# Fewer, differently shaped side transfers in the recurrent layer of a four-layer graph network

## The chip, the cores and the metric

The kernel runs on one core of a Trainium2 chip. The metric is device time in microseconds (us) of one execution. Before the change it is 3273.84 us, the median of three runs (3273.52 to 3274.08).

## The reference, cut to what matters

The network takes x (64 graphs, 256 nodes, 256 features) and adj (64 x 256 x 256), in float32, and applies four layers, each of the form x = layernorm(x + layer(x)). Only layer 0 is touched by the change. It is a recurrence over the 256 nodes: the state of a node is computed from the states that are there, and replaces its row before the next node is computed.

```python
d = jnp.sum(adj, axis=-1)
dinv = jnp.where(d != 0, 1.0 / jnp.where(d != 0, d, 1.0), 0.0)
norm_adjT = jnp.swapaxes(adj, 1, 2) * dinv[:, :, None]
def step(h, i):
    x = jnp.take(h_e, i, axis=1)
    row = jnp.take(norm_adjT, i, axis=1)
    x_par = jnp.einsum('bj,bjd->bd', row, h)
    iou = x @ W_ioux.T + b_ioux + x_par @ W_iouh.T + b_iouh
    r, z = jnp.split(iou, 2, axis=1)
    r, z = (jax.nn.sigmoid(r), jax.nn.sigmoid(z))
    hc = jnp.tanh(x @ W_coux.T + b_coux + x_par * r @ W_couh.T + b_couh)
    h_new = z * x_par + (1.0 - z) * hc
    h = jax.lax.dynamic_update_slice(h, h_new[:, None, :], (0, i, 0))
    return (h, None)
```

So each step needs, for each of the 64 graphs, a weighted sum x_par over all nodes: original features for nodes from here on, new states for nodes already done. Layers 1 to 3 (a graph convolution and two attention layers) follow.

## The kernel before, in words

`_recurrence` is layer 0, and `_layers` runs the other three. The 256 steps are one Python loop, `for now in range(N)`, unrolled into an instruction list whose order is written out by hand: every engine, and the queue of SyncE (SP), executes its instructions in exactly the order of the program. n is the step, p = n % 8 its place in a group of eight (U = 8), k and i = divmod(n, 32) its block of 32 (T = 32) and the place in it. State tiles hold two halves of the features (256 = 2 x 128) over 64 graphs, so 128 partitions.

**The chain of a step.** The weighted sum xp is transposed (`flip`, L627 on TensorE, L629 on ScalarE), multiplied with the weights (`h_part`, L620), goes through the sigmoid (L861, used here as the mark at which a step begins), a transpose and a product (L863, L865), a second product, tanh (L898), zcc (L900), and ends in the next xp (L903). Everything else is fitted beside this chain.

**The weighted sum** of a step is assembled in a tile ACC of its group from five sources:
- the original features: products of x_side, written to HBM (Us) and loaded by `sums_in` (L316, at p = 1);
- the recent states: VectorE adds them one by one (`push`, L645) or ScalarE and GpSimd in groups (`scale_far`, L687 to L696);
- the window of states before that: `late`. States are kept in a ring Hw (128 partitions, one for each of 64 recent nodes and half of the graphs), written by `into_ring` (L672 to L676), two transfers a state. At p = 0 to 3 of a group, TensorE multiplies Hw with a table An (L531), ScalarE copies the products into lb (L256), and lb goes to HBM and back into another partition order: `send` (L511, two transfers Lb<-lb) and `receive` (L517, late_sb<-Lb). GpSimd adds late_sb to the ACC of the next group at p = 6 and 7 (L909);
- older states: `early`. Blocks of states are flushed to HBM (`flush`, L655, Hd<-Hw, at i = 8 and 16), loaded again together with adj, multiplied at p = 4 to 7 (L424), copied into a tile eu, and stored: `store` (L436, two transfers Es<-eu), called by `at_step` one step after the last copy. `early_in_part` (L453) loads them at p = 0 for the group after the next, as one transfer of 128 partitions x 8 x 128, and GpSimd adds them at p = 3 and 4 (L855);
- the node's own value, with a table Sd.

**Tables.** While block k runs, the tables of k + 1 are prepared: `degrees` loads rows of adj (L301, two transfers of 256 KB each time) and sums them on VectorE (L304, two reductions for each load), called as a generator at the values of i in a tuple; `late_load` loads a raw table from adj (at most four transfers for a block) and GpSimd cuts An out of it at n + 15 to 23; `load_S` loads S.

**The queue.** All transfers of the loop go through SP's one in-order queue, at the end of each step: first those filed under this step by `at_step` (`transfers`), then `early_in_part`, `sums_in`, the next x (xq), flush, degrees, raw and S, and, at p < 4, up to two loads from the list `loads` (`load_later`, `next_load`, L269), sorted by a rank. The ring inserts are issued in the middle of a step, at p = 4 to 7: at most two states a step, that is, four transfers:

```python
if p > 3 or n >= N - U:
    for _ in range(min(2, len(ring_in))):
        into_ring()
```

The `late` products of a group at p = 0 read the ring with the states of the group before it, up to the one that is finished at the start of p = 7; that one is in the last two transfers of p = 7.

Of the kernel before, what the change touches and what calls it, by code (L numbers as in the profile page):

```python
# [9 lines left out]
F32 = mybir.dt.float32  # L10
# [9 lines left out]
P = 128  # L20
# [50 lines left out]
def _recurrence(tc, ident, Hd, x, adj, W_ioux, b_ioux, W_iouh, b_iouh, W_coux, b_coux, W_couh, b_couh, wide, then):  # L71
# [19 lines left out]
    nc = tc.nc  # L91
    B, N, D = x.shape
    T = 32
# [10 lines left out]
    with ExitStack() as ctx:  # L104
# [149 lines left out]
        def copy_later(out, in_, then=None):  # L254
            def f(n):
                nc.scalar.copy(out, in_)  # L256
                held.pop(0)
                if then:
                    then(n)

            copies.append(f)
# [118 lines left out]
        def early_load(n, k, lo, hi, t):  # L380

            rows = hi - lo
            if (k, lo) not in Es:
                Es[k, lo] = dram.tile([2, NG, 4, T, P], F32, name=f"Es_{k}_{lo}", bufs=1)
            if not any(e[0] == (hi, t) for e in states_in):
                Hs = wide.tile([P, GB, D], F32, tag="wide", name=f"Hs_{hi}_{t}")
                states_in.append(((hi, t), Hs, load_later(
                    Hs[0:rows], Hd[lo:hi, t * GB:(t + 1) * GB, :], 1
                )))
            _, Hs, begun = next(e for e in states_in if e[0] == (hi, t))  # L390
            if t % 2 == 0:
                A = stream.tile([P, 2 * GB, T], F32, tag="A", name=f"A_{k}_{lo}_{t}")
                early_A[:] = A, load_later(
                    A[0:rows],
                    adj[t * GB:(t + 2) * GB, lo:hi, k * T:(k + 1) * T].rearrange("b j i -> j b i"), 1
                )
            early_in.append(((begun, early_A[1]), k, lo, hi, t, Hs, early_A[0]))
# [14 lines left out]
        def early_fill(n):  # L412

            if early_pb:
                pb, e = early_pb.pop(), 1
            else:
                if not early_in or not landed(early_in[0][0], n):
                    return False
                _, k, lo, _, t = early_in[0][0:5]
                pb, e = base_bank([P, 2, D], f"early_{k}_{lo}_{t}"), 0  # L420
                early_pb.append(pb)
            _, k, lo, hi, t, Hs, A = early_in[0]
            for q in range(4):
                nc.tensor.matmul(  # L424
                    pb[q * T:(q + 1) * T, e, :], A[0:hi - lo, t % 2 * GB + e * 4 + q, :],
                    Hs[0:hi - lo, e * 4 + q, :], start=True, stop=True,
                )
            if e:
                early_in.pop(0)
                if t % 2 == 0:  # L430
                    early_ub[:] = [stream.tile([P, 4, D], F32, tag="ub", name=f"eu_{k}_{lo}_{t}")]
                ub = early_ub[0]

                def store():
                    for c in range(2):
                        nc.sync.dma_start(  # L436
                            Es[k, lo][c, 2 * t - 2:2 * t + 2].rearrange("n q i f -> (q i) n f"),
                            ub[:, :, c * P:(c + 1) * P],
                        )

                copy_later(
                    ub[:, t % 2 * 2:t % 2 * 2 + 2, :], pb,
                    (lambda n: at_step(n + 1, store)) if t % 2 else None,
                )
            return True

        def early_in_part(first):

            k, i = divmod(first, T)
            for (kk, lo), E in Es.items():  # L450
                if kk == k:
                    part = blk.tile([P, U, P], F32, tag="early", name=f"early_sb_{first}_{lo}")
                    nc.sync.dma_start(  # L453
                        part, E[:, :, :, i:i + U, :].rearrange("c n q i f -> (c n q) i f")
                    )
                    early_parts.append((first, part))

        early_parts = []

        def late_load(k, n=None):  # L460


            An = blk.tile([P, HB, U, T // U], F32, tag="An", name=f"An_{k}")
            raw = stream.tile([P, HB, T], F32, tag="raw", name=f"raw_{k}", bufs=1)
            first, last = k * T - W + T // 2, k * T + T // 2
            if first < 0:
                nc.gpsimd.memset(raw, 0.0)
            begun = []
            for lo, hi, at in ring(max(first, 0), last):
                for g in range(2):  # L470
                    to = raw[g * W + at:g * W + at + hi - lo]
                    of = adj[g * HB:(g + 1) * HB, lo:hi, k * T:(k + 1) * T].rearrange(
                        "b j i -> j b i"
                    )
                    if n is None:
                        nc.scalar.dma_start(to, of)
                    else:
                        begun.append(load_later(to, of, 1.5))

            def begin():  # L480
                while not all(begun):
                    next_load(now)

            def cut(lo):
                part = raw[:, lo:lo + HB // 4].rearrange("p b (s u) -> p b s u", u=U)
                take = window[k % 2].rearrange("p (s u) -> p s u", u=U).unsqueeze(1)
                nc.gpsimd.tensor_mul(
                    An[:, lo:lo + HB // 4].rearrange("p b u s -> p b s u"), part,
                    take.to_broadcast(list(part.shape)),
                )  # L490

            if n is not None:
                at_step(n + 12, begin)
            for e in range(4):
                if n is None:
                    cut(e * HB // 4)
                else:
                    at_step(n + (15, 18, 21, 23)[e], lambda e=e: cut(e * HB // 4))
            return An

        def late(first):

            k, i = divmod(first, T)
            An = tables[k]["An"]
            lb = stream.tile([P, NG, D], F32, tag="lb", name=f"lb_{first}", bufs=1)
            Lb = dram.tile([2, NG, 4, U, P], F32, tag="Lb", name=f"Lb_{first}")
            sides[first] = blk.tile([P, U, P], F32, tag="late", name=f"late_sb_{first}", bufs=1)

            def send():
                for c in range(2):  # L510
                    nc.sync.dma_start(  # L511
                        Lb[c].rearrange("n q u f -> (q u) n f"),
                        lb[i // U::T // U, :, c * P:(c + 1) * P],
                    )

            def receive():
                nc.sync.dma_start(sides[first], Lb.rearrange("c n q u f -> (c n q) u f"))  # L517
# [6 lines left out]
            for u in range(0, NG // 2, 2):  # L524
                pb = [base_bank([P, 2, D], f"late_{first}_{u}_{g}") for g in range(2)]
                for e in range(2):
                    for q in range(4):
                        for g in range(2):
                            rows = slice(g * W, (g + 1) * W)
                            b = (u + e) * 4 + q  # L530
                            nc.tensor.matmul(  # L531
                                pb[g][q * T:(q + 1) * T, e, :],
                                An[rows, b].rearrange("p u s -> p (u s)"),
                                Hw[rows, b, :], start=True, stop=True,
                            )
                    if e:
                        for g in range(2):
                            at = g * NG // 2 + u
                            copy_later(
                                lb[:, at:at + 2, :], pb[g],  # L540
                                then if g and u + 2 == NG // 2 else None,
                            )
                    n = yield
# [157 lines left out]
        sums = {}  # L701
        sides = {}
        xqT = {}
        pushes = []
        ring_in = []

# [42 lines left out]
        warm = work.tile([P, P], F32, tag="ready", name="warm", bufs=1)[:, 0:1]  # L749
        nc.vector.memset(warm, 0.0)  # L750
        nc.scalar.activation(warm, warm, AF.Sigmoid)
        tables[0]["An"] = late_load(0)
        tables[0]["Sd"] = chain_S(0)
        for a in range(1, 3):
# [38 lines left out]
        for now in range(N):  # L793
# [10 lines left out]
            if n:  # L804
# [11 lines left out]
                    behind = [(n - 1, hs, m, 4) for m in range(end, min(end + U, N), 4)]  # L816

                if p > 3 or n >= N - U:
                    for _ in range(min(2, len(ring_in))):
                        into_ring()  # L820
            if p == 0 and U < n + U < N:
                late_side = late(n + U)
# [109 lines left out]
            if k + 1 < NB:  # L932
                if i == 0:
                    background = degrees(k + 1)
                for _ in range((0, 2, 3, 3, 8, 10, 11, 15, 16, 17, 20, 21, 23, 24).count(i)):
                    next(background, None)
                if i == 0:
                    tables[k + 1]["S"], double = load_S(k + 1, n)
                    at_step(n + 19, double)
                    tables[k + 1]["An"] = late_load(k + 1, n)  # L940
                if i == 28:
                    tables[k + 1]["Sd"] = chain_S(k + 1)
            if p < 4:
# [623 lines left out]
```

## Time and profile before

| what | us |
|---|---|
| time, median of three runs | 3273.84 |
| the profiled execution | 3276.55 |
| its span in the profile | 3274.8 |
| steps of the recurrence, first to last sigmoid (L861) | 137.1 to 1432.9 |
| TensorE busy in the span | 3071.4 |
| VectorE, ScalarE, GpSimd busy in the span | 2587.5, 1990.7, 1881.9 |

The profile is of one execution. A line of a view names an engine, a line of the kernel and the tile written and read, for instance "late<-Hw,An". SPq is the queue of SP; its lines are issues of transfers, whose data land later. In a timeline the columns are start, duration, engine, line, operation and tiles, a count, and in brackets how long the engine stood idle before and what ended it. In a table of windows each row is a stretch of time: its length, the busy time of TensorE, of its weight loads, of VectorE, ScalarE and GpSimd, with counts of instructions, then TensorE's clock, the mean busy share of the 16 DMA engines, and GB/s.

A step takes about 5.6 us at p = 0, 5.2 at p = 4 and 4.4 to 4.7 elsewhere; 38.8 us for an undisturbed group of eight.

### The profile page before, as it was taken

The numbers are of one execution on the slowest core, as the hardware profiler recorded it, in microseconds if no ns is written. First come the engines' busy times: TensorE is split into PE (matmuls) and PEld (weight loads), VectorE is DVE, ScalarE is ACT, GpSimd is POOL, SyncE is SP. The second block draws the span as 40 slices with busy tenths as digits, with TensorE's granted clock in tenths as the row PEclk, the third lists the DMA queues.
The fourth block names the chain that finished last, engine by engine and source line by source line (L and its number), as shares of the span: only waits on it lengthen the run. The fifth ranks groups of instructions, "written<-read, shape, count | busy, mean of one in ns | idle before, by whom it ended". The sixth has DMA issues, their size and how long they took to land.

```text
span 3274.8 us, 80656 instructions
## 1 busy us (share of the span) xinstructions
PE 3071.4 (94%) x28332; PEld 2275.9 (69%) x28332; DVE 2587.5 (79%) x7361; ACT 1990.7 (61%) x5224; POOL 1881.9 (57%) x2226
## 2 busy tenths in 40 slices
PE   4799999999899989959999999999999999999997
PEld 3566666555565555647888888888888888888885
DVE  2477777777678778756888988888888888888885
ACT  0266666666566656635666666666666666666664
POOL 2366767766677778733555555555555555555543
PEclk8899999999999999978999999999999999999999
DMA  9866777687776764433333333333333333333310
GB/s 297 258 163 148 188 176 185 166 180 183 175 184 148 181 152 139 100 72 70 78 78 78 78 78 78 78 78 78 78 78 78 78 79 77 79 77 78 78 43 21
DMA packets 806736, 385.77 MB, mean 118 GB/s; under 512 B 525260, under 2 KB 774232, under 8 KB 802648
## 3 DMA queue, kind: packets, MB, share of 16 engines
q1 hardware_dynamic: 788312, 362.61, 46.4%
q10 hardware_dynamic: 18016, 17.96, 1.7%
q8 instruction: 227, 3.72, 0.5%
q14 instruction: 181, 1.48, 0.2%
HBM read 261.75 MB, written 99.61 MB: 110 GB/s over the span
## 4 chain that ended last, share of the span: by engine, by line
PE 82%; DMA 7%; DVE 6%; issue 2%; SPq 2%; POOL 1%; ACT 1%; ACTq 0%; DVEq 0%; POOLq 0%
PE mm L1044 14%; PE rc L620 7%; PE rc L612 5%; PE s L1270 4%; PE late L531 4%; PE mm_3v L1044 4%; PE mm_2f L1044 4%; PE mm_2v L1044 3%; PE mm_3f L1044 3%; PE mm_t L1044 3%; PE mm_g L1044 3%; PE mm_2s L1044 3%; PE mm_2w L1044 3%; PE o L1305 3%; PE z_ps L620 2%; PE z_ps L612 2%
## 5 line engine op out<-in xcount | busy, mean ns | idle before, releaser
L1282 POOL TENSOR_TENSOR p3s<-p 128x256 f32<-128x256 f32 x512 | 358.4, 732 | 269.5 <-ACT p L1280 269.3
L1044 PE MATMUL mm<-xT,weights 128*128 128x256 f32 x2048 | 485.4, 385 | 2.7 <-ACT xT L1160 2.7
L696 POOL TENSOR_TENSOR ACC<-ACC,far 128x640 f32<-128x640 f32 (+2 forms) x312 | 412.8, 1323 | 69.8 <-ACT far L687 26.1
L645 DVE SCALAR_TENSOR_TENSOR ACC<-keep,S,ACC 128x128 f32<-128x128 f32 x1561 | 436.8, 343 | 13.0 <-POOL ACC L909 8.2
L1044 PEld LDWEIGHTS mm<-xT,weights 128*128 128x128 f32 x2048 | 387.1, 192 | 80.4 <-ACT xT L1160 29.3
L1279 DVE TENSOR_TENSOR p<-s,neg 128x512 f32<-128x512 f32 x512 | 317.7, 683 | 84.8 <-PE s L1270 84.8
L1000 ACT ACTIVATE y<-y,shift,rstd 128x256 f32<-128x256 f32 x512 | 279.6, 596 | 158.2 <-DVE shift L998 158.1
L1280 ACT ACTIVATE p<-p 128x512 f32<-128x512 f32 x512 | 307.0, 629 | 3.1 <-DVE p L1279 3.0
L612 PE MATMUL rc<-WxT,xqT 128*64 128x256 f32 x2048 | 271.8, 387 | 2.2 <-ACT xqT L256 2.2
L842 POOL TENSOR_TENSOR ready<-ACC,dinv 128x128 f32<-128x128 f32 x255 | 101.8, 399 | 279.6 <-DVE ACC L645 275.1
L992 POOL TENSOR_TENSOR rstd<-rstd,mhalf 128x2 f32<-128x2 f32 x256 | 173.5, 695 | 134.2 <-DVE rstd L991 132.4
L692 POOL TENSOR_TENSOR far<-hs,S 128x384 f32<-128x384 f32 (+1 forms) x310 | 222.0, 716 | 4.7
L1319 DVE RECIPROCAL rT<-o 128x256 f32<-128x256 f32 x128 | 223.7, 1748 | 0.0
L988 DVE BATCH_NORM_STATS2 st<-y 128x6 f32<-128x256 f32 x512 | 209.6, 409 | 12.7 <-POOL y L1181 9.9
L1192 ACT ACTIVATE qk<-mm,weights 128x256 f32<-128x256 f32 x256 | 107.5, 471 | 164.1 <-PE mm L1044 162.2
L1181 POOL TENSOR_TENSOR y<-y,g 128x512 f32<-128x512 f32 x64 | 81.1, 1267 | 216.7 <-ACT g L1178 190.2
L531 PE MATMUL late<-Hw,An 64*32 64x256 f32 x3840 | 166.3, 402 | 35.7 <-DMA Hw<-hs 21.5
L620 PE MATMUL rc<-WhT,rT 128*64 128x128 f32 x2048 | 172.3, 290 | 26.2 <-DVE rT L865 24.5
L620 PE MATMUL rc<-WhT,xpT 128*64 128x128 f32 x2048 | 170.9, 288 | 25.7 <-ACT xpT L629 24.5
L620 PEld LDWEIGHTS rc<-WhT,rT 128*64 128x64 f32 x2048 | 109.0, 138 | 123.7 <-DVE rT L865 102.5
L687 ACT ACTIVATE far<-hs,S 128x128 f32<-128x128 f32 x534 | 183.7, 397 | 3.1 <-POOL ACC L696 0.8
L620 PEld LDWEIGHTS rc<-WhT,xpT 128*64 128x64 f32 x2048 | 107.8, 137 | 106.1 <-ACT xpT L629 95.7
(170 smaller groups left out, 7307.8 us busy)
## 6 DMA issues: line engine op xcount, KB each, us to landing
xX<-in_x_dram ACTq DMA_DIRECT2D x16, 1024.0 KB
Us<-xu SPq DMA_DIRECT2D x64, 256.0 KB
ACC<-Us SPq DMA_DIRECT2D x32, 512.0 KB
Es<-eu SPq DMA_DIRECT2D x64, 256.0 KB
early_sb<-Es SPq DMA_DIRECT2D x32, 512.0 KB
xin<-in_x_dram SPq DMA_DIRECT2D x64, 256.0 KB
ad<-in_adj_dram SPq DMA_DIRECT2D x64, 256.0 KB
y<-Hd SPq DMA_DIRECT2D x64, 256.0 KB
```

Of the source, the lines that this page charges most:

```text
L531: nc.tensor.matmul(pb[g][q * T:(q + 1) * T, e, :], An[rows, b].rearrange("p u s -> p (u s)"), Hw[rows, b, :], start=True, stop=True,)
L612: nc.tensor.matmul(G[o * B:(o + 1) * B], xqT[a, i // 2][:, i % 2, kc, h * B:(h + 1) * B], WxT[:, kc, o, gates], start=False, stop=False, s ...
L620: nc.tensor.matmul(G[o * B:(o + 1) * B], hT[:, kc * B:(kc + 1) * B], WhT[:, kc, o, g], start=False, stop=(kc == 1), skip_group_check=True,)
L645: nc.vector.scalar_tensor_tensor(acc[:, 0, :], keep[:, j % 2, :], s, acc[:, 0, :], ALU.mult, ALU.add)
L692: nc.gpsimd.tensor_mul(tmp[:, begun:count, :], hs.unsqueeze(1).to_broadcast(shape), s[:, begun:count].unsqueeze(2).to_broadcast(shape),)
L696: nc.gpsimd.tensor_add(acc, acc, tmp[:, 0:count, :])
L1000: nc.scalar.activation(y[:, c, :], y[:, c, :], AF.Identity, bias=shift[:, c:c + 1], scale=rstd[:, c:c + 1],)
L1044: nc.tensor.matmul(pm[:, c, :], lhsT[:, k, c * P:(c + 1) * P], rhs[:, k, :], start=(k == 0), stop=(k == 1),)
L1279: nc.vector.tensor_add(p, s_ps[i], self.neg3)
L1280: nc.scalar.activation(p, p, AF.Exp, scale=ISQ)
L1282: nc.gpsimd.tensor_add(both, p[:, 0, :], p[:, 1, :])
L1319: nc.vector.reciprocal(rT, o_ps[:, 1, :])
```

## The change

Five edits, all in layer 0's side work:
1. lb and eu are laid out as [2 halves][units][128] rather than [units][256], so that the two transfers of `send` and of `store` become one each, with the same bytes. The copies on ScalarE write into the new layout.
2. Es in HBM is laid out in the order [pair of units][half][4][4][32][128]. `early_in_part` becomes two transfers of 64 partitions each, one for each half. The outermost dimension of each source is the 4 of the pairs.
3. `store` is filed one step later when its last copy falls in a step with p = 5 (p = 7 rather than 6).
4. The raw table is loaded by a function of its own, `raw_load`, called at i = 24 of the block before (n = 0 for the second block), rather than at i = 0; of the four loads of degree rows in a block, the second moves from i = 3 to i = 8, and its two reductions from i = 8 and 10 to i = 10 and 11; the third load stays at i = 11.
5. Ring inserts take up to 3, 3, 1 and 1 states at p = 4, 5, 6 and 7, rather than two each time.

```diff
-                Es[k, lo] = dram.tile([2, NG, 4, T, P], F32, name=f"Es_{k}_{lo}", bufs=1)
+                Es[k, lo] = dram.tile([NG // 4, 2, 4, 4, T, P], F32, name=f"Es_{k}_{lo}", bufs=1)
...
-                    early_ub[:] = [stream.tile([P, 4, D], F32, tag="ub", name=f"eu_{k}_{lo}_{t}")]
+                    early_ub[:] = [stream.tile([P, 2, 4, P], F32, tag="ub", name=f"eu_{k}_{lo}_{t}")]
...
                 def store():
-                    for c in range(2):
-                        nc.sync.dma_start(
-                            Es[k, lo][c, 2 * t - 2:2 * t + 2].rearrange("n q i f -> (q i) n f"),
-                            ub[:, :, c * P:(c + 1) * P],
-                        )
-
+                    nc.sync.dma_start(
+                        Es[k, lo][t // 2].rearrange("c n q i f -> (q i) (c n) f"),
+                        ub.rearrange("p c n f -> p (c n) f"),
+                    )
+
+                at = t % 2 * 2
                 copy_later(
-                    ub[:, t % 2 * 2:t % 2 * 2 + 2, :], pb,
-                    (lambda n: at_step(n + 1, store)) if t % 2 else None,
+                    ub[:, :, at:at + 2, :].rearrange("p c n f -> p n c f"),
+                    pb.rearrange("p n (c f) -> p n c f", c=2),
+                    (lambda n: at_step(n + (2 if n % U == 5 else 1), store)) if t % 2 else None,
                 )
...
                     part = blk.tile([P, U, P], F32, tag="early", name=f"early_sb_{first}_{lo}")
-                    nc.sync.dma_start(
-                        part, E[:, :, :, i:i + U, :].rearrange("c n q i f -> (c n q) i f")
-                    )
+                    for c in range(2):
+                        nc.sync.dma_start(
+                            part[c * B:(c + 1) * B],
+                            E[:, c, :, :, i:i + U, :].rearrange("e n q i f -> e (n q) i f"),
+                        )
...
-            lb = stream.tile([P, NG, D], F32, tag="lb", name=f"lb_{first}", bufs=1)
+            lb = stream.tile([P, 2, NG, P], F32, tag="lb", name=f"lb_{first}", bufs=1)
...
             def send():
-                for c in range(2):
-                    nc.sync.dma_start(
-                        Lb[c].rearrange("n q u f -> (q u) n f"),
-                        lb[i // U::T // U, :, c * P:(c + 1) * P],
-                    )
+                nc.sync.dma_start(
+                    Lb.rearrange("c n q u f -> (q u) (c n) f"),
+                    lb[i // U::T // U].rearrange("p c n f -> p (c n) f"),
+                )
...
-                    for _ in range(min(2, len(ring_in))):
+                    for _ in range(min((3, 3, 1, 1)[p - 4] if n < N - U else 2, len(ring_in))):
                         into_ring()
...
-                for _ in range((0, 2, 3, 3, 8, 10, 11, 15, 16, 17, 20, 21, 23, 24).count(i)):
+                for _ in range((0, 2, 3, 8, 10, 11, 11, 15, 16, 17, 20, 21, 23, 24).count(i)):
                     next(background, None)
                 if i == 0:
+                    if not k:
+                        raw_load(1, n)
                     tables[k + 1]["S"], double = load_S(k + 1, n)
                     at_step(n + 19, double)
                     tables[k + 1]["An"] = late_load(k + 1, n)
+                if i == 24 and k + 2 < NB:
+                    raw_load(k + 2, n)
```

More of the change, by code (lines that the diff above doesn't have):

```diff
@@ L452, in early_in_part, with raw_load @@
                     part = blk.tile([P, U, P], F32, tag="early", name=f"early_sb_{first}_{lo}")
-                    nc.sync.dma_start(
-                        part, E[:, :, :, i:i + U, :].rearrange("c n q i f -> (c n q) i f")
-                    )
+                    for c in range(2):
[3 more added lines that the diff above has]
+                        )
                     early_parts.append((first, part))
         early_parts = []
-        def late_load(k, n=None):
-            An = blk.tile([P, HB, U, T // U], F32, tag="An", name=f"An_{k}")
+        def raw_load(k, n=None):
             raw = stream.tile([P, HB, T], F32, tag="raw", name=f"raw_{k}", bufs=1)
@@ L478, in late_load @@
                         begun.append(load_later(to, of, 1.5))
+            raws[k] = raw, begun
+        def late_load(k, n=None):
+            An = blk.tile([P, HB, U, T // U], F32, tag="An", name=f"An_{k}")
+            raw, begun = raws.pop(k)
             def begin():
@@ L539, in late @@
                             copy_later(
-                                lb[:, at:at + 2, :], pb[g],
+                                lb[:, :, at:at + 2, :].rearrange("p c n f -> p n c f"),
+                                pb[g].rearrange("p n (c f) -> p n c f", c=2),
                                 then if g and u + 2 == NG // 2 else None,
@@ L703, in _recurrence @@
         xqT = {}
+        raws = {}
         pushes = []
@@ L751, in _recurrence @@
         nc.scalar.activation(warm, warm, AF.Sigmoid)
+        raw_load(0)
         tables[0]["An"] = late_load(0)
```

## The prediction

> **What bounds the kernel now.** I read the page first, then the waits, then one stalled group in the timelines of TensorE and SP, then the DMA share by step.
>
> Only layer 0 changes, 1296 us from its first to its last sigmoid. TensorE is nearly always busy there, but each step is a chain through TensorE, ScalarE and VectorE, so what counts is how far a step is over its normal length. I took the time between sigmoids (L861) for all steps: undisturbed p = 0 steps take 5.60, yet those that begin at 671, 758, 841, 887 and 1170 us take 12.21, 11.09, 12.66, 11.95 and 12.10. Their excess is 6.61 + 5.49 + 7.06 + 6.35 + 6.50 = 32.0 us; smaller ones, at n = 32, 48, 72, 88, 152, 168, 176, 184 and 208, add 15. What do the stalled steps wait for?
>
> The page's row of the late products, and the answer on their line, of which two rows say what TensorE waited for:
>
> ```profile
> L531 PE MATMUL late<-Hw,An 64*32 64x256 f32 x3840 | 166.3, 402 | 35.7 <-DMA Hw<-hs 21.5
> ...
>   DMA Hw<-hs: 32.2, 16
>   issue: 28.6, 48
> ```
>
> Ring inserts are the release in 16 stalls of 32.2 us. In the timeline of TensorE round 671 us the wait stands between the transpose of the sigmoid and the first late product (it is put down to Es, which had landed last; the ring's last insert went out just before it):
>
> ```profile
> 671.28 0.33 PE L863 MATMUL rT_ps<-ident,rs 128*128 128x128 f32 x1
> 675.65 1.11 PE L531 MATMUL late<-Hw,An 64*32 64x256 f32 x16 [4.05 <-DMA Es<-eu]
> ```
>
> And SP's timeline of the same group, whole from the send of lb to the early load:
>
> ```profile
> 652.22 1.46 SPq L511 DMA_DIRECT2D Lb<-lb  x2
> 653.78 1.25 SPq L301 DMA_DIRECT2D rows<-in_adj_dram  x2
> 655.07 1.76 SPq L269 DMA_DIRECT2D raw<-in_adj_dram  x2
> 656.94 2.33 SPq L676 DMA_DIRECT2D Hw<-hs  x4
> 659.37 0.67 SPq L517 DMA_DIRECT2D late_sb<-Lb  x1
> 660.09 6.68 SPq L676 DMA_DIRECT2D Hw<-hs  x8
> 666.87 1.46 SPq L436 DMA_DIRECT2D Es<-eu  x2
> 668.42 2.76 SPq L676 DMA_DIRECT2D Hw<-hs  x4
> 671.29 1.51 SPq L436 DMA_DIRECT2D Es<-eu  x2
> 672.85 0.69 SPq L453 DMA_DIRECT2D early_sb<-Es  x1
> ```
>
> The last insert is out at 671.18, 0.24 us after the sigmoid (670.94); the product starts 4.5 us later, where it normally starts 0.76 us after the sigmoid. In undisturbed groups the last insert is out 4.3 to 4.5 us before it, soon after its state exists. So SP's queue is the bound of these groups, and it is late because inserts begin 14.0 us before the sigmoid and not 18 to 19: the queue is still working off what p = 0 to 3 piled up. The table of windows, steps p = 0 to 3 of the group at 802 us, then a step with little but ring inserts:
>
> ```profile
> 801.90:807.50 5.60, 5.50 (x96) 3.11 (x94) 3.74 (x14) 3.74 (x12) 4.69 (x6) 1.00 1.11 272
> 807.50:812.20 4.70, 4.70 (x80) 2.93 (x78) 3.72 (x14) 3.52 (x12) 4.08 (x5) 1.00 1.03 250
> 812.20:816.90 4.70, 4.70 (x80) 2.93 (x76) 4.23 (x15) 3.39 (x11) 2.29 (x3) 1.00 0.99 231
> 816.90:821.70 4.80, 4.76 (x72) 2.93 (x68) 4.55 (x17) 3.70 (x13) 3.88 (x5) 1.00 1.08 237
> ...
> 1281.50:1285.90 4.40, 3.66 (x48) 2.58 (x46) 3.64 (x14) 2.39 (x9) 3.49 (x5) 1.00 0.14 43
> ```
>
> The last columns are DMA share and GB/s: for 20 us all 16 engines are full. 14 groups with an early load (n = 48, 56, 64, 80, 96, 104, 112, 128, 136, 144, 152, 160, 176, 192) have a share near 1 over most of p = 0 to 4.
>
> **What the Trainium skill says.** "DMA: Bandwidth & Descriptors", section "Why a DMA increments its semaphore by 16 and not by 1": a transfer issued by SP runs on the largest k up to 16 that divides the slowest dimension of both access patterns, on the lowest-numbered k engines. The trace agrees: ring inserts have an outermost 2, and share 0.14 above is 2/16 = 0.125. Section "Rules for kernel authors": two transfers to disjoint halves of the partitions bring nothing, use one; and an outermost dimension under 16 confines a transfer. The change follows the first for Lb and Es, and goes against both with the early load. Section "Queues, rings and completion order": each engine consumes its descriptors in ring order, so a transfer behind a narrow one is held up on the narrow one's engines. No view here shows a four-engine transfer.
>
> **The change part by part.** TensorE's and GpSimd's instructions and their order stay; on VectorE seven reductions of 0.68 us each move.
>
> *Lb, Es, p = 7.* Two issues of 1.46 become one, about 0.73. The store at 666.87 moves behind the last insert: 1.55 us less ahead of it. Where a group has one, its inserts end 1.5 + 0.7 = 2.2 us earlier.
>
> *Raw and the second degree rows* leave the groups that end at i = 8: in the group shown, 1.25 + 1.76 and gaps, 3.2 us more. (Raw issues one step earlier, at 641.7, lasted 10.4 us; they mostly waited for the full engines.) First insert: 656.9 - 0.7 - 3.2 = 653.0, or 18 before the sigmoid, as in undisturbed groups; from first to last 14.2 - 1.5 = 12.7, so the last ends at 665.7, before the floor of -4.4. Stalls at 104, 136 and 200 go, with 72 and 168: 6.61 + 7.06 + 6.50 + 1.1 + 1.8 = 23.1 us. Raw arrives at i = 24 instead: there 2.4 us of issue against the 2.2 saved, some +0.4 at 88, 120, 152, 184: +1.6. Remaining groups (32, 144, 176, 208, 48) gain up to 2.05 each: 1.66 + 2.05 + 0.7 + 0.65 + 1.0 = 6.1. Sum -27.6.
>
> *Given back.* late_sb now stands behind six inserts, not four: +1.4 for two issues, -0.7 for Lb. GpSimd's L909 waited for it 9.8 us in 7 groups; 7 x 0.7 = 5 more; queued behind L909 is the next step's "ready". The second rows stand right behind the flush, whose two transfers of 512 KB land 3.3 to 4.4 us each, and VectorE wants them at the end of i = 10: 0 to 5 us each in up to five blocks; I take 1 each, 5. When stalls at i = 8 are gone, p = 0 to 3 of the next group find the engines full sooner: of 6.6 and 7.1 us I let 40% come back, 5. Sum +15, so net -12.6; with the store's later release of its eu buffer (two groups) nothing more, at most +2.
>
> *Copies* to lb and eu (304 at 0.59): strided, same elements. Bounds 0 and +0.06 each, 18 us if nothing hid it; they end behind tanh, so 0. *3, 3, 1, 1* by itself: floor unchanged, the last state is the last either way; 0, counted in late_sb.
>
> *The early load.* Before: 128 rows of 4 KB on 16 engines, 8 rows each; landings in the saturated stretches are 1.24 us apart, 0.155 a row. After: two transfers with an outermost 4, so four engines, 16 rows each: 2 x 16 x 0.155 = 5.0 us on engines that all later transfers use too. Lag +3.7 us a load, +7.4 where two blocks' loads stand together (n = 176 to 232). GpSimd wants the data at p = 3, some 16 us later: no stall there. The harm is behind it: flush, S, x, then the first inserts, which use two of these four engines. In stalled groups (104, 136, 144, 152) the lag counts whole: 4 x 3.7 = 14.8. In the eight others with single loads about 2 us disappear in the shorter chain of inserts: 8 x 1.7 = 13.6. At 176 and 192, 2 x (7.4 - 2) = 10.8. Sum 39 if all of it reaches the chain; bounds 0 and 39. p = 5 to 7 have free engines and SP's issues may be the limit anyway, so I take 60%: +23.5.
>
> Net -12.6 + 23.5 = +11: 3276.55 + 11 = 3287.5 for a profiled execution. That lies 2.7 above the median before, so I predict 3285.
>
> **The rivals.**
> *Absorbed lag (ends faster).* The four-engine load delays others, but the lag is worked off at p = 4 to 7, where the share falls to 0.3 to 0.5, before the inserts matter; or the rule gives this pattern more engines. Then -12.6, or up to -27.6 with nothing given back: 3261 to 3246, taken 3259. For: share 0.27 to 0.36 at p = 6. Against: inserts are needed from p = 4 on, at share 0.8 to 0.9. It decides once under a third of the lag passes: 12.6/39 = 0.32, 1.2 us a load.
> *Balance.* Stalls move from ring to late_sb and rows, gain and loss within 6.5 us: 3274.
> *Whole lag and late rows.* +39 - 12.6 and another 10 to 20 at VectorE: 3300 to 3320, taken 3310.
> *The change does not do what it says:* order of instructions shows all five edits; only the number of engines is open, counted in the first.
>
> **How the numbers follow.** Forecast 0.38 (own range 3278 to 3300), absorbed lag 0.37, balance 0.13, whole lag 0.12. 0.2%, 6.5 us, is about what a measurement tells from no change. Faster 0.36, same 0.15, slower 0.49. The range 3248 to 3310 leaves out the ends of the fastest and the slowest case.
>
> **What would show it.** Right: p = 0 steps at n = 104, 136, 200 near 5.6 us; early transfers with four engines, and DMA share near 0.25 more where nothing else runs; in groups from 48 to 192 first inserts later than 18 us before the sigmoid, waits for Hw or late_sb at other groups. Wrong: early landings 1.2 us apart (rule fails), or first inserts unmoved (lag absorbed), then faster; reductions L304 waiting for rows over 2 us each would mean the worst case.

## The result: 1.55% slower

The changed kernel takes 3326.01 us (median of four runs, 3322.31 to 3328.20) against 3273.68 us (3270.90 to 3274.08) for the kernel before: a ratio of 1.0155, with a 95% interval of 1.0140 to 1.0170. The forecast, 3285 us, had the sign, not the size: the loss is 52 us where 11 were forecast, and the time lies outside the range of 3248 to 3310.

The stalls that the prediction began with are gone. The groups of the changed kernel, in the columns of the page (busy time and mean; idle time before, with the releases that ended most of it):

```profile
L538 PE MATMUL late<-Hw,An 64*32 64x256 f32 x3840 | 162.7, 392 | 8.4 <-DMA Hw<-hs 2.9 <-DMA early_sb<-Es 1.9 <-POOL ready L852 0.9
...
L919 POOL TENSOR_TENSOR ACC<-ACC,late_sb 128x512 f32<-128x512 f32 x60 | 76.2, 1270 | 43.7 <-DMA late_sb<-Lb 41.4
...
L304 DVE TENSOR_REDUCE deg<-rows 128x2 f32<-128x512 f32 x56 | 38.1, 680 | 21.7 <-DMA rows<-in_adj_dram 21.7
```

TensorE's idle time at the late products fell from 35.7 us to 8.4. But GpSimd now stands 41.4 us for late_sb, and VectorE 21.7 us for degree rows. In the kernel before, the same two groups read:

```profile
L909 POOL TENSOR_TENSOR ACC<-ACC,late_sb 128x512 f32<-128x512 f32 x60 | 76.3, 1272 | 12.2 <-DMA late_sb<-Lb 9.8
...
L304 DVE TENSOR_REDUCE deg<-rows 128x2 f32<-128x512 f32 x56 | 38.0, 679 | 0.0
```

Taken step by step over the recurrence, the changed kernel less the kernel before, by p from 0 to 7: -41.6, +3.8, +7.5, +30.5, +9.0, +3.7, +0.4 and +37.9 us; together +51.2. So 41.6 us were won at p = 0, more than forecast, and 93 lost elsewhere: most of it at p = 3, where VectorE waits for rows before it may write the state, and at p = 7, where GpSimd's wait for late_sb holds back ACC. SP's timeline of the group that ends at 687 us answers the one in the prediction:

```profile
665.28 6.29 SPq L518 DMA_DIRECT2D Lb<-lb  x1
671.68 3.77 SPq L684 DMA_DIRECT2D Hw<-hs  x6
675.80 0.35 SPq L524 DMA_DIRECT2D late_sb<-Lb  x1
676.21 8.67 SPq L684 DMA_DIRECT2D Hw<-hs  x10
684.98 2.06 SPq L435 DMA_DIRECT2D Es<-eu  x2
687.10 2.06 SPq L455 DMA_DIRECT2D early_sb<-Es  x2
689.20 0.95 SPq L663 DMA_DIRECT2D Hd<-Hw  x2
690.20 4.32 SPq L301 DMA_DIRECT2D rows<-in_adj_dram  x1
```

The store of Es stands behind the inserts, and the last insert goes out at 684.9, 2.2 us before the sigmoid at 687.1: the product follows 1.6 us after it instead of 4.7. But the inserts still begin late, 15.4 us before the sigmoid: the issue of Lb ahead of them took 6.29 us. SP's wait there is put down to ScalarE, whose copies fill lb, and not to the DMA engines.

Two stalls as the timelines of the changed kernel show them, of VectorE and of GpSimd:

```profile
705.84 0.69 DVE L304 TENSOR_REDUCE deg<-rows 128x2 f32<-128x512 f32 x1 [4.69 <-DMA rows<-in_adj_dram]
706.44 0.28 DVE L674 TENSOR_TENSOR keep<-zcc,keep 128x128 f32<-128x128 f32 x1
...
947.93 1.26 POOL L919 TENSOR_TENSOR ACC<-ACC,late_sb 128x512 f32<-128x512 f32 x1 [5.80 <-DMA late_sb<-Lb]
```

Each engine runs in order, so the new state (L674) waits 4.69 us behind a reduction that nothing else is in a hurry for, and that step takes 11.33 us where it took 4.77 before. The second stall makes its step 12.26 us where it took 4.51.

So the steps are 6.56 and 7.75 us longer, more than the waits of 4.69 and 5.80. The rest is TensorE, whose products run slower after a stall. The same eight products in an undisturbed step of the changed kernel, and after the first of the two stalls:

```profile
223.84 0.66 PE L628 MATMUL rc<-WhT,rT 128*64 128x128 f32 x8
...
708.85 1.12 PE L628 MATMUL rc<-WhT,rT 128*64 128x128 f32 x8 [4.21 <-DVE rT L875]
```

And the whole recurrence as one window, in the kernel before and in the changed one:

```profile
137.10:1432.90 1295.80, 1203.53 (x15954) 769.31 (x15952) 973.26 (x3444) 815.38 (x2716) 922.39 (x1049) 0.98 0.67 161
...
135.90:1482.90 1347.00, 1225.92 (x15954) 786.19 (x15952) 975.75 (x3444) 814.28 (x2717) 922.37 (x1049) 0.96 0.65 155
```

The same 15954 products keep TensorE busy 22.4 us longer, so of the 51.2 us about 22 are slower products and 29 are idle time. The traces record when TensorE had half its clock: 11 stretches, 56 us, in the recurrence of the kernel before, and 18, 104 us, in that of the changed one. Each of them begins in a gap of TensorE of 1.5 to 5.0 us or less than 2.5 us after one. What lowers the clock, and from what gap on, no run here shows.

### The profile page after: what moved, and what is told of

Its sections match the earlier page's. It is cut to its first block, busy times and chain, and to the rows that moved or that the text cites. A ratio compares the mean times of both kernels' runs of the same rounds, so it can differ in the third digit from the quotient of the medians.

```text
span 3324.6 us, 80591 instructions
## 1 busy us (share of the span) xinstructions
PE 3091.5 (93%) x28332; PEld 2290.5 (69%) x28332; DVE 2587.3 (78%) x7361; ACT 1988.3 (60%) x5224; POOL 1882.1 (57%) x2226
## 4 chain that ended last, share of the span: by engine, by line
PE 76%; DMA 10%; DVE 6%; SPq 3%; issue 2%; POOL 1%; ACT 1%; ACTq 0%; DVEq 0%; POOLq 0%
PE mm L1058 14%; PE rc L628 6%; PE rc L620 4%; PE s L1284 4%; PE mm_3v L1058 4%; PE mm_2f L1058 4%; PE mm_2v L1058 3%; PE mm_3f L1058 3%; PE mm_t L1058 3%; PE mm_g L1058 3%; PE mm_2s L1058 3%; PE mm_2w L1058 3%; PE o L1319 3%; PE late L538 3%; DMA rows<-in_adj_dram 3%; DVE ACC L653 2%
## 5 line engine op out<-in xcount | busy, mean ns | idle before, releaser
L653 DVE SCALAR_TENSOR_TENSOR ACC<-keep,S,ACC 128x128 f32<-128x128 f32 x1561 | 436.8, 343 | 40.1 <-POOL ACC L919 35.5
L620 PE MATMUL rc<-WxT,xqT 128*64 128x256 f32 x2048 | 279.4, 395 | 2.2 <-ACT xqT L256 2.2
L875 DVE TENSOR_TENSOR rT<-rT_ps,xpT 128x128 f32<-128x128 f32 x256 | 74.2, 290 | 153.8 <-PE rT_ps L873 151.0
```

Source lines behind the costliest of these rows:

```text
L620: nc.tensor.matmul(G[o * B:(o + 1) * B], xqT[a, i // 2][:, i % 2, kc, h * B:(h + 1) * B], WxT[:, kc, o, gates], start=False, stop=False, s ...
L653: nc.vector.scalar_tensor_tensor(acc[:, 0, :], keep[:, j % 2, :], s, acc[:, 0, :], ALU.mult, ALU.add)
```

## The experiments

The first four runs ask two questions: do the four-engine loads cause these waits, or would the transfers of p = 0 to 3 bring them once the stall at p = 0 is gone? And did the move of the rows, or the 3, 3, 1, 1, make its own wait?

**The changed kernel with the wide early load.**

```diff
-  Es[k, lo] = dram.tile([NG // 4, 2, 4, 4, T, P], ...)
+  Es[k, lo] = dram.tile([2, NG, 4, T, P], ...)
...
-  nc.sync.dma_start(Es[k, lo][t // 2]..., ub...)
+  for c in range(2):
+      nc.sync.dma_start(Es[k, lo][c, 2 * t - 2:2 * t + 2].rearrange("n q i f -> (q i) n f"), ub[:, c])
...
-  for c in range(2):
-      nc.sync.dma_start(part[c * B:(c + 1) * B], E[:, c, ...].rearrange("e n q i f -> e (n q) i f"))
+  nc.sync.dma_start(part, E[:, :, :, i:i + U, :].rearrange("c n q i f -> (c n q) i f"))
```

> The changed kernel with Es laid out as before: one early load of 128 partitions, and the store in two transfers again (still filed a step later for p = 5); Lb, raw, degree rows and 3, 3, 1, 1 as changed. Theory A, the four-engine early loads hold up what is queued behind them, and with it late_sb and the degree rows: most of the 68 us of new waits at p = 3 and p = 7 go, the gain at p = 0 stays: 3258 to 3280 us. Theory B, the transfers of p = 0 to 3 take their time anyway, and a stall removed at p = 0 comes back as a wait at p = 3 or 7 whatever the early load does: 3310 to 3330.

Measured: ratio 0.9978 to the kernel before (0.9967 to 0.9989), 3264.91 us, in the range of theory A. The second edit taken back, and with it the single store of Es, turns 1.55% slower into 0.22% faster. Its waits for rows fall to 1.7 us, those for late_sb to 25.3, and p = 0 stays mended (13.8 us of excess, that is, of time above the length of undisturbed steps, against 49.5 in the kernel before).

**The kernel before with the narrow early load alone.**

```diff
-  Es[k, lo] = dram.tile([2, NG, 4, T, P], ...)
+  Es[k, lo] = dram.tile([NG // 4, 2, 4, 4, T, P], ...)
...
-  Es[k, lo][c, 2 * t - 2:2 * t + 2].rearrange("n q i f -> (q i) n f")
+  Es[k, lo][t // 2, c].rearrange("n q i f -> (q i) n f")
...
-  nc.sync.dma_start(part, E[:, :, :, i:i + U, :].rearrange("c n q i f -> (c n q) i f"))
+  for c in range(2):
+      nc.sync.dma_start(part[c * B:(c + 1) * B], E[:, c, ...].rearrange("e n q i f -> e (n q) i f"))
```

> The kernel before with only the layout of Es and the early load changed: two transfers of 64 partitions with an outermost 4; the stores stay two transfers, at their old steps. A: 3300 to 3325 us, stalls at p = 0 longer in the groups from 48 to 200. B: within 10 us of the kernel before (3264 to 3284), since the load is hidden.

Measured: ratio 1.0174 (1.0153 to 1.0195), 3328.68 us, 57 us more than before and just above A's range. The narrow load alone, with its stores in two transfers, makes the whole loss. So theory A holds in both directions, and theory B falls as the main cause; a remnant of it stays in the 25.3 us for late_sb of the version with the wide load, against 9.8 before. But the second half of A's expectation was wrong: the stalls at p = 0 hardly changed (50.1 us of excess against 49.5). Its groups show where the loss is:

```profile
L911 POOL TENSOR_TENSOR ACC<-ACC,late_sb 128x512 f32<-128x512 f32 x60 | 76.2, 1270 | 37.9 <-DMA late_sb<-Lb 35.5
...
L304 DVE TENSOR_REDUCE deg<-rows 128x2 f32<-128x512 f32 x56 | 38.1, 680 | 1.9 <-DMA rows<-in_adj_dram 1.5 <-issue 0.4
```

**How a transfer on four engines holds up the others.** That the narrow transfers run on four engines shows in the semaphore events: each has four landings after its issue, where each of two wide ones, in a version below, has 16. The prediction thought of the order on these four engines. SP's waits show a second way. First the kernel before, then the changed one, in columns: line, what it waited for, us in total, times, longest.

```profile
SPq L269 <- DMA early_sb<-Es: 2.0, 2, 1.3
SPq L316 <- DMA early_sb<-Es: 0.4, 1, 0.4
SPq L582 <- DMA early_sb<-Es: 0.4, 1, 0.4
```

```profile
SPq L269 <- DMA early_sb<-Es: 24.0, 11, 3.8
SPq L316 <- DMA early_sb<-Es: 13.1, 7, 3.8
SPq L590 <- DMA early_sb<-Es: 10.4, 4, 4.3
```

These issues need nothing from early_sb. Transfers issued by SP take turns on eight semaphores, as the instruction list has it, and the ninth waits until the first of the eight has landed. So a slow early load also stops the issue of what follows it: 47.5 us in total against 2.8. But it isn't shown that this makes the loss. None of these waits of the changed kernel lies between 617 and 959 us, where three of its longest stalls are (steps n = 107, 119 and 151), and over all of them together the DMA share is 0.81, so the engines mostly stay at work (1.09 in the one at 482.7 us, 0.53 in the one at 1134.3).

Elsewhere the engines do run low beside an early load. These are p = 0 and p = 1 of the group at 821 us of the changed kernel, whose counterparts in the kernel before, in the prediction, have shares of 1.11 and 1.03:

```profile
821.30:828.00 6.70, 5.55 (x96) 3.16 (x92) 3.68 (x14) 3.82 (x13) 4.66 (x6) 1.00 0.80 214
828.00:832.70 4.70, 4.70 (x80) 2.93 (x76) 3.83 (x14) 3.50 (x13) 4.19 (x5) 1.00 0.52 123
```

The two early loads go out at 821.12 and 822.84 and have landed at 830.22 and 832.64. SP stands behind them in one issue:

```profile
825.26 7.15 SPq L269 DMA_DIRECT2D Hs<-Hd  x1
```

The profile names nothing that ends this issue. And a low share alone proves little: the kernel with the wide load has a step with 0.35, at 898.8 us, while SP waits for GpSimd. No run changes the number of semaphores, so how much of the 57 us comes through the order on the four engines, and how much through SP's issue, stays open.

**The second degree rows loaded at i = 3 again**, in the changed kernel.

```diff
-  for _ in range((0, 2, 3, 8, 10, 11, 11, 15, 16, 17, 20, 21, 23, 24).count(i)):
+  for _ in range((0, 2, 3, 3, 8, 10, 11, 15, 16, 17, 20, 21, 23, 24).count(i)):
```

> The changed kernel with the second degree rows loaded at i = 3 again. The new waits of VectorE for rows at i = 11 (n = 75, 107, 139, 171, 203) add to 18 us of excess over before. If the move made them: 3305 to 3311. If the rows only show a lag that is there anyway (A): the waits come at other places, those at i = 3 (n = 67 and 195) stay or grow, and the time is 3316 to 3330.

**Two states inserted in each step**, in the changed kernel.

```diff
-  for _ in range(min((3, 3, 1, 1)[p - 4] if n < N - U else 2, len(ring_in))):
+  for _ in range(min(2, len(ring_in))):
```

> The changed kernel with two states inserted in each of p = 4 to 7. late_sb stands behind four inserts and not six, 1.3 us earlier. If the place of late_sb among the inserts made the waits of GpSimd at p = 7 (38 us of excess over before): 3290 to 3300. If late_sb is late because the queue ahead of p = 4 is (A): about 1.3 us in each of some 10 groups, 3310 to 3320, and some of it back at p = 0.

Measured: 1.0147 (1.0114 to 1.0180) and 1.0159 (1.0136 to 1.0182): neither can be told from the changed kernel's 1.0155. Rows at 3316.72 fit the reading of a lag that is there anyway; two inserts at 3324.78 gain less than either reading gave them. The traces show why. With the rows back, the excess at p = 3 falls from 30.2 to 13.5 us and that at p = 7 rises from 51.8 to 62.5. With two inserts a step, p = 7 falls from 51.8 to 28.1 and p = 0 and p = 3 rise, from 9.0 to 24.0 and from 30.2 to 39.6. The excess adds to 126.7 us in the changed kernel, 124.7 and 127.8 in these two, and 133.8 in the kernel before with the narrow load. While the queue is that late, an edit of the order only chooses which consumer waits.

**Number of transfers or number of engines?** Two more versions of the kernel before: the early load in two transfers of 64 partitions over contiguous rows,

```diff
-  nc.sync.dma_start(part, E[:, :, :, i:i + U, :].rearrange("c n q i f -> (c n q) i f"))
+  for c in range(2):
+      nc.sync.dma_start(part[c * B:(c + 1) * B], E[c, :, :, i:i + U, :].rearrange("n q i f -> (n q) i f"))
```

> The kernel before with the early load in two transfers of 64 partitions over contiguous rows, so 16 engines each; the layout of Es as before. It tells the number of transfers from the number of engines. If the engines made the loss: within 6 us of the kernel before (3266 to 3278), the second transfer landing about 0.6 us after the first. If two transfers and their issue (32 more, 0.6 us each) made it: 3290 or more.

and one with only the second of the two narrow (Es in two tensors, the second with a gap after every four units, so that its outermost dimension stays 4):

```diff
-  Es[k, lo] = dram.tile([2, NG, 4, T, P], ...)
+  Es[k, lo] = [dram.tile([NG // 4, 1, 4, 4, T, P], ...), dram.tile([NG // 4, 2, 4, 4, T, P], ...)]
...
+  for c in range(2):
+      nc.sync.dma_start(part[c * B:(c + 1) * B], E[c][:, 0, ...].rearrange("e n q i f -> e (n q) i f"))
```

> The kernel before with the early load in two transfers, the first over contiguous rows (16 engines), the second with an outermost 4 (four engines): some 0.6 + 2.5 us of a load rather than 2 x 2.5, that is, half of the lag of the kernel with both halves narrow, which took 57 us more. If each us of lag costs the same: +25 to +32, 3297 to 3304. If the groups have slack for a lag of 2 us: +0 to +12, 3272 to 3284.

| early load, in the kernel before | ratio (95%) | SP's waits for early_sb, us | GpSimd's for late_sb, us |
|---|---|---|---|
| one transfer, 16 engines | 1 | 2.8 | 9.8 |
| two, 16 and 16 | 1.0038 (1.0026 to 1.0050) | 4.2 | 14.2 |
| two, 16 and 4 | 1.0111 (1.0091 to 1.0131) | 23.1 | 25.1 |
| two, 4 and 4 | 1.0174 (1.0153 to 1.0195) | 46.9 | 35.5 |

From row to row the ratio grows by 0.0038, 0.0073 and 0.0063: about 12, 24 and 21 us. Each narrow half costs much the same, so there is no slack that takes the first 2 us of lag; the version with one narrow half came out at 36 us, above its +25 to +32. TensorE's busy time in the recurrence grows down the table too, 1203.5, 1214.3, 1216.5 and 1230.3 us, so nearly half of the 57 us are slower products. Two wide transfers, at 3288.90, lie between the two readings, near the other one's 3290: the number of transfers makes up to a fifth of the loss, 12 of 57 us, which was expected to be nothing; the number of engines makes the rest. In the semaphore events of the traces the second of two early transfers landed a median of 0.96 us after the first with two wide ones, 2.66 with the second one narrow and 2.72 with both.

**Which of the other edits help once the load is wide?** All of these start from the changed kernel with the wide load (ratio 0.9978); only the lines named differ.

```diff
-  min((3, 3, 1, 1)[p - 4] if n < N - U else 2, len(ring_in))
+  min(2, len(ring_in))
```

> The changed kernel with the wide early load, and two states inserted in each of p = 4 to 7. In the kernel with the wide load and 3, 3, 1, 1, GpSimd waits 25 us for late_sb, against 10 before. If that comes from the six inserts ahead of late_sb: 12 to 15 us of it go, and some 5 come back at p = 0: 3253 to 3260. If the waits only change place, as in the kernel with narrow loads: 3262 to 3270.

```diff
-  at_step(n + (2 if n % U == 5 else 1), store)
+  at_step(n + (2 if n % U == 5 and n > 80 else 1), store)
```

> The changed kernel with the wide early load, ring inserts 3, 3, 1, 1 as changed, and the store a step later only after n = 80. It parts the two edits of the kernel with 2, 3, 2, 1, which was 6.5 us under the one with the wide load alone. If the buffer's release made it (waits of ScalarE for Es at n = 39 and 71): 3256 to 3261. If the order of inserts made it: 3262 to 3268.

```diff
-  at_step(n + (2 if n % U == 5 else 1), store)
+  at_step(n + (2 if n % U == 5 and n > 80 else 1), store)
...
-  min((3, 3, 1, 1)[p - 4] if n < N - U else 2, len(ring_in))
+  min((2, 3, 2, 1)[p - 4] if n < N - U else 2, len(ring_in))
```

> The changed kernel with the wide early load, ring inserts of 2, 3, 2, 1 states (late_sb behind four inserts, one state left for p = 7), and the store of Es a step later only after n = 80, so that the first groups' buffer comes free as before. Expected: the waits for late_sb as before (10 us), those of ScalarE for Es at n = 39 and 71 gone (5 us): 3248 to 3258. If waits only change place: 3262 to 3270.

and from that last one, the edits of the change taken back:

```diff
-  for _ in range((0, 2, 3, 8, 10, 11, 11, 15, 16, 17, 20, 21, 23, 24).count(i)):
+  for _ in range((0, 2, 3, 3, 8, 10, 11, 15, 16, 17, 20, 21, 23, 24).count(i)):
```

> The kernel with wide load and 2, 3, 2, 1, its second degree rows loaded at i = 3 again. With wide loads VectorE hardly waits for rows at i = 11, so the move should be worth little either way: 3255 to 3264. If it had cleared the queue ahead of the inserts at i = 8: stalls at p = 0 of n = 104, 136 and 200 come back in part, 3264 to 3270.

```diff
                 if i == 0:
-                    if not k:
-                        raw_load(1, n)
                     tables[k + 1]["S"], double = load_S(k + 1, n)
                     at_step(n + 19, double)
+                    raw_load(k + 1, n)
                     tables[k + 1]["An"] = late_load(k + 1, n)
-                if i == 24 and k + 2 < NB:
-                    raw_load(k + 2, n)
```

> The kernel with wide load and 2, 3, 2, 1, the raw table loaded at i = 0 again. If raw made the stalls at i = 8 (n = 104, 136, 200: 6.6, 7.1 and 6.5 us in the kernel before): most of 20 us come back at p = 0, less some 8 that the next groups then don't wait, 3266 to 3274. If Lb, Es and the inserts alone took them away: 3255 to 3262.

Both together:

> The kernel with wide load and 2, 3, 2, 1, raw and the second degree rows both where they were before. What is left is one transfer for Lb, the later store and the order of inserts. If raw and rows are the gain: 3270 to 3276, as the kernel before. If the single Lb and the later Es store are: 3256 to 3264.

| kernel, all with the wide load | ratio (95%) | median, us |
|---|---|---|
| 3, 3, 1, 1, all else as changed | 0.9978 (0.9967 to 0.9989) | 3264.91 |
| 2, 2, 2, 2 | 0.9973 (0.9960 to 0.9986) | 3266.44 |
| 3, 3, 1, 1, later store only after n = 80 | 0.9957 (0.9944 to 0.9970) | 3259.33 |
| 2, 3, 2, 1, later store only after n = 80 | 0.9944 (0.9924 to 0.9965) | 3258.47 |
| the same, rows at i = 3 | 0.9969 (0.9960 to 0.9978) | 3264.11 |
| the same, raw at i = 0 | 0.9966 (0.9956 to 0.9976) | 3262.38 |
| the same, rows at i = 3 and raw at i = 0 | 0.9972 (0.9964 to 0.9980) | 3266.47 |

Two inserts a step missed their 3253 to 3260: the wait for late_sb was to shrink by 12 to 15 us, the time did not move, as the other reading had it. The early release of the store's buffer brings some 0.2%, with intervals that just touch: ScalarE's waits for Es fall from 7.3 us to 3.0, and that run met its expectation. With 2, 3, 2, 1 beside it, a further 0.1% that the intervals don't tell apart; that version came out just above its 3248 to 3258, with 17.2 us of waits for late_sb where 10 were expected. Rows and raw taken back cost some 0.2% each, with intervals that overlap, and no more together. None of the three falls squarely in a reading: rows at 3264.11 on the border of the two, raw at 3262.38, 4 us dearer and not the 8 to 16 that were expected if it made the stalls at i = 8, both at 3266.47 between the two. With both back, 0.28% of gain is left for the single Lb, the later store and the order of inserts; the other half may be rows' and raw's, though the two intervals just touch.

The version with 2, 3, 2, 1 beats both kernels: 0.56% under the kernel before, 2.1% under the changed one. GpSimd's and TensorE's groups in it:

```profile
L537 PE MATMUL late<-Hw,An 64*32 64x256 f32 x3840 | 161.8, 392 | 18.8 <-DMA Es<-eu 7.0 <-DMA Hw<-hs 5.9 <-DMA Us<-xu 1.8
...
L918 POOL TENSOR_TENSOR ACC<-ACC,late_sb 128x512 f32<-128x512 f32 x60 | 76.3, 1271 | 19.6 <-DMA late_sb<-Lb 17.2
```

It waits at both places, 18.8 and 19.6 us, and at neither as long as one of the two kernels does.

## Why the prediction was wrong, step by step

**The bound before and what the change does to it: right.** Stalls at n = 104, 136 and 200 fell from 12.21, 12.66 and 12.10 us to 6.47, 5.60 and 5.60. The gain at p = 0, put at 27.6, was 41.6. The 32.2 us that the prediction gives to the ring in 16 stalls hold 10.7 us of weight loads; the products wait 21.5 us, as the page's row says.

**The early load: number of engines and time of one transfer right.** "Two transfers with an outermost 4, so four engines", 2.5 us for each: in the changed kernel the second lands a median of 2.68 us after the first. The rule of the Trainium skill on the number of engines, in "DMA: Bandwidth & Descriptors", section "Why a DMA increments its semaphore by 16 and not by 1", gave the four engines, and the traces agree: each narrow transfer has four landings. The rule against two transfers to halves of the partitions, which the prediction also quotes, is about the early load; Lb and Es were two halves of the columns, so it says nothing of them.

**The step that failed is the price of the early load.** The prediction let a lag of 39 us in all reach the chain at most, took 60% of it, 23.5, and put splitting the load in two, apart from the engines, at nothing. Measured alone, the narrow load costs 57, of which up to 12 come with two transfers even when both are wide. Four things were amiss:
- It counted 14 groups, those with a DMA share near 1, and took 2 us off in most of them. By its own 3.7 us a load the lag of all 32 loads would be 118 us, an estimate, and 57 is 48% of that.
- It let the lag count whole in groups that were stalled (104, 136, 144, 152) and less in the others. It is the other way round. In the kernel before with the narrow load, those four groups together are 5.9 us shorter, while the five groups that begin a block (64, 96, 128, 160, 192) are 43 us longer. One reading is that during a stall the transfers land under no pressure, while a group at full speed has no such cover. Another is that the groups that begin a block have the loads of raw, S and rows behind the early load. No run parts the two.
- It looked for the harm at the ring inserts. It came at late_sb (35.5 us against 9.8) and at the A tables (11.0 us of TensorE's waits at the early products, against 2.8), and SP's own waits for early_sb, 46.9 us, were not in the prediction.
- It counted a us of lag as at most a us of time. With the narrow load alone TensorE's busy time grows by 26.8 us for the same products: new stalls bring slower products with them.

**The other edits, -12.6: about half, and partly by luck.** With the wide load they give 0.22%, 7 us. In the profiled executions 36.7 us are won there at p = 0, where 27.6 were forecast, and 27.3 come back at the other steps, where 15 were: two errors of much the same size. With the narrow load they give 1.0174 less 1.0155, 0.19%, which the intervals don't tell from nothing or from 0.22%. Measured apart, the two parts add: +57 and -7 make +50, against the 52 of the change. So the sum was right to add them; its terms were wrong, and the early load's by far the most.

**late_sb and the rows, +5 each: late_sb too small.** With the wide load, which leaves the other edits, they measure 15.5 us (25.3 less 9.8) and 1.7. In the changed kernel they are 31.6 and 21.7. Of the first the narrow load alone gives 25.7; the second needs both, the moved rows and the narrow load, which alone gives 1.5. Each was priced from its two issues and the flush ahead of it, as if the queue before it stayed as it was. The worst rival, 3310, named the lag and the rows; it too was 16 us short.

**The raw load and the rows, 23.1 us with their share of the store: too large.** Together they bring 0.28%, 9 us, in the version with the wide load.

## What to carry to other kernels

When two edits touch one queue, measure each alone: here two runs, -7 and +57 us, take the 52 apart. A wait taken away at one consumer can come back at others: here 27 us of 37. When a transfer is re-shaped, look at the outermost dimension of both patterns first, and then at what the queue issues behind it. Price a stall with the slower products after it: here they were 22 us of 51. If moving things about in a queue only moves the wait from one consumer to another, leave the order alone and look for the transfer that wastes engines.

## What the runs showed of the hardware that was not expected

Splitting a wide transfer into two wide ones of half the size cost 0.38% here, 32 more transfers a run. In the profiled execution 4.4 us of the difference lie before n = 48, where no early load has been issued, so they are not the early load's. Most of them are one step, n = 32: TensorE waits 2.39 us for the ring there, against 1.63 in the kernel before, and the eight products after the wait take 1.12 us, against 0.66, so that the step takes 10.71 us against 7.26. At n = 17 TensorE stops inside a group of eight products for 2.00 us against 0.85, with nothing in the profile that ends the wait. In the changed kernel that stop lasts 2.73 us and again slower products follow: steps 17 and 18 take 7.98 and 7.29 us, against 5.85 and 4.69. What causes the stop wasn't found.

All other versions are longer than the kernel before in this stretch, by 3 to 11 us. So a difference of a few us between two versions, 0.1 or 0.2%, need not come from the edit that parts them.
